# Loads behind the offset conv, the norm's mean and root one product later, and other orders in the first and last slots of a deformable bottleneck

## The chip, the cores and the metric

The kernel runs on one core of a Trainium2 chip. The metric is the device time in microseconds (us) of one execution. TensorE is called PE here, VectorE DVE, ScalarE ACT, GpSimd POOL and SyncE SP, as in the profile. All data are float32.

## The reference, cut to what matters

Two residual bottlenecks run one after the other on x of shape (64, 1024, 14, 14).

```python
# layer 0: batch norms over the whole batch
out = relu(bn(conv1x1(x, w1) + b1))            # 1024 -> 256
out = relu(bn(conv3x3(out, w2) + b2))          # 256 -> 256
x = relu(x + softplus(scale) * bn(conv1x1(out, w3) + b3))
# layer 1: group norms with 32 groups per image, a deformable 3x3 conv
out = relu(gn(conv1x1(x, w1)))                 # 1024 -> 256
om = conv3x3(out, w_off) + b_off               # 27: offsets x, y and a mask, 9 taps each
sampled = bilinear(out, grid + offsets) * sigmoid(mask)     # 9 taps x 256 channels
out = relu(gn(sum over taps of w2[tap] @ sampled[tap]))
return relu(gn(conv1x1(out, w3)) + x)          # 256 -> 1024
```

## The kernel before, in words

Two images make a pair; there are 32 pairs (NP), and a pair's 392 positions are the columns of a matmul. Layer 0 runs until about 967 us and leaves its third conv's results (h3) in DRAM, because its last batch norm needs all pairs. Layer 1 finishes layer 0's last norm, residual and ReLU pair by pair and then does its own work. The change touches layer 1 alone (`build_second_bottleneck`) and a helper for its weights.

Layer 1 is a pipeline over slots. `fill()` (from about 967 us) brings pairs 0 and 1 in and starts pair 2; then `slot(t)` runs for t = 0 to 31, and `tail()` ends pair 31. In slot t the following work of several pairs is laid side by side:

- the first conv of pair t+1 (`first_conv`, L1092, 16 matmuls) with the norm of pair t-1's second conv (`second_norm`) placed between its products, the store of the second half of pair t-2 (`output(t-2, 1)`, L1752), and `load(t+2)`, which issues four DMAs on SP: x into Y[(t+2) % 4] (L196) and h3 into Z0 (L204);
- the sampling of pair t (`sampling`, L1396 on PE, copied by ACT at L1404 into the sample tiles sm_0 with five taps and sm_1 with four), woven with pair t-1's third conv (`third_conv`, L1640), whose sums V, E and z are made by DVE and POOL (L1647 to L1660) and whose last statistics are taken by DVE at L987;
- the offset conv of pair t+1 (`offset_conv`) and `selection` (L1219 to L1234), which ends with DMAs of offsets, weights and mask (dm, wt, mk) through DRAM and back;
- the second conv of pair t (`second_conv`, L1511). It is a 2x2 block product in seven products instead of eight, in the order 5, 0, 4, 1, 2, 3, 6, with five taps in its first part (pd[0], 35 steps) and four in its second (pd[1], 28 steps). A step is one product of 196 columns. DVE makes the differences of sample halves that it needs (L1467): the first (b12 - b11) comes from `first_sum`, tied to program order; three more are issued at steps of the conv. `finish_second` copies the bank E by ACT (L1535), and DVE adds V (L1539) and the outputs h (L1542, 1543, 1549), of which it takes statistics for gn_2.

Between the steps of pd[0] stand, each before a step's number: the mean of pair t-1's third norm at 4, its root at 10 and its scale at 20; `first_sum(t, 0)` at 4 and `first_sum(t, 1)` at 20; the transposes of pair t+1 at 6, 11, 16 and 21 (L1283); its interpolation weights (`factors`, L1246 to L1266, which ends with DMAs wd) at 12 and 19; and `residual(t+2)` at 21 (eight DVE adds at L216 and eight ReLUs of ACT at L228). A norm (`Norm`) is: `total` (m from the statistics, DVE L1003), `mean` (PE L1012, then gm, q and v on DVE, L1014 to L1026), `root` (PE L1031, DVE L1036, a power on POOL L1037) and `scale` (sc, sh; DVE L1043 to L1053). The third norm is then applied to z by ACT in 16 pieces (L1707). In the profile its tiles have the name gn_0, and the norm of the second conv in the next slot has a name with the pair's number, gn_29 for instance.

Two more parts belong to the change. `spread_rows` and `spread_columns` (L1324, L1359) gather wd from DRAM into tiles S and X, and `corners` (L1376) multiplies them on DVE. The last pair (31) uses `plain_second_conv` (L1431), which has two outputs o with two inputs c each, 392 columns, and one difference of a whole sample tile by DVE (L1428) ahead of output 1. In `fill`, `sums_of_second` makes sums of the second conv's weights on DVE (L911).

What sets the order: PE's instructions in layer 1 run in the order in which the code emits them (`tc.manual_schedule` for PE). Lists of steps are put together by `weave` and by `put(steps, extra, at)`, which emits each extra ahead of the step with its number; extras with the same number keep their order in the list after a stable sort. The other engines' order is set by a scheduler, apart from instructions wrapped in `tc.keep_in_program_order`, which stay in the emitted order among each other. A program that also handles far offsets (FULL) is in the kernel, but its branch isn't taken.

Of the kernel before, what the change touches and what calls it, by code (L numbers as in the profile page):

```python
# [20 lines left out]
CB = 8  # L21
HB = CB // 2
MB = 2
T = 9
# [20 lines left out]
def kernel(  # L45
# [854 lines left out]
    Sc = {n: const.tile([P, T, P], FP, tag=f"Sc{n}", name=f"Sc{n}") for n in (1, 2, 4)}  # L900
    Sc[3] = c21

    def sums_of_second():
        for k in range(0, T, 3):
            for n, a, b, op in (
                (1, c21, c22, ALU.add),
                (2, Sc[1], c11, ALU.subtract),
                (3, c11, c21, ALU.subtract),
                (4, c12, Sc[2], ALU.subtract),
            ):  # L910
                nc.vector.tensor_tensor(Sc[n][:, ds(k, 3)], a[:, ds(k, 3)], b[:, ds(k, 3)], op)  # L911


    omax = const.tile([32, NP], FP, tag="omax", name="omax")
# [9 lines left out]
    def build_second_bottleneck(l1, path, run, early):  # L924
# [144 lines left out]
        def load(p):  # L1069
            start(p)  # L1070

            load_x(p, tc.keep_in_program_order)
            load_h3(p, Z0, tc.keep_in_program_order)

        def residual(p):

            for b in range(CB):

                tc.keep_in_program_order(end_of_first(p, Z0, b))
                relu_of_first(p, b)  # L1080
# [251 lines left out]
        def spread_columns(p, e):  # L1332

            q = pairs[p]
            k0, k1 = tapsets[e]
            n = wide * KT[e % 2]
            if shared and p == e == 0:


                first, second = (  # L1340
                    two.tile([P, HB, N2], FP, tag="z", name=f"X_{n}").rearrange("p b n -> p (b n)")
                    for n in range(2)
                )

                cut = [piece for _, _, piece in pieces(e)][-1].start
                where = lambda piece: (
                    second[:QR, : piece.stop - cut] if piece.start == cut else first[:QR, piece]
                )
            elif shared:
                t = sample_buffer(e, f"X_{p}_{e}")  # L1350
                where = lambda piece: t[:QR, piece]
                if e == 1:
                    transformed[p + 1] = t[:, n:]
            else:
                t = one.tile([QR, n], FP, tag=f"X{e % 2}", name=f"X_{p}_{e}")
                where = lambda piece: t[:, piece]
            q["X"][e] = where
            for g, r0, piece in pieces(e):
                yield nc.sync.dma_start(  # L1359
                    where(piece),  # L1360
                    q["wd"][g][1, :, k0:k1, :]
                    .rearrange("r k n -> r (k n)")
                    .unsqueeze(0)
                    .to_broadcast([R, W, piece.stop - piece.start]),
                )
# [49 lines left out]
        def plain_second_conv(p, e):  # L1415


            q = pairs[p]
            k0, k1 = tapsets[e]

            def step(k, o, c):
                sm = q["sm"][e]
                if k == o == c == 0:
                    q["pd"] = [
                        ps_d.tile([P, N2], FP, tag=f"pd{n}", name=f"pd_{p}_{n}") for n in range(MB)
                    ]
                if (k, o, c) == (k0, 1, 0):
                    nc.vector.tensor_tensor(  # L1428
                        sm[:, 1, : k1 - k0], sm[:, 1, : k1 - k0], sm[:, 0, : k1 - k0], ALU.subtract
                    )  # L1430
                nc.tensor.matmul(  # L1431
                    q["pd"][o],
                    ((c11, c12), (Sc[1], c22))[o][c][:, k],
                    sm[:, c, k - k0].rearrange("p i q -> p (i q)"),
                    start=(k == 0 and c == 0),
                    stop=(k == T - 1 and c == MB - 1),
                )
                if k == T - 1 and c == MB - 1:
                    if o == 0:
                        outputs_of_second(p)  # L1440
                    nc.scalar.copy(q["h2"][:, o, :], q["pd"][o])
                    second_stats(p, o)

            return [
                lambda a=(k, o, c): step(*a)
                for o in range(MB)
                for k in range(k0, k1)
                for c in range(MB)
            ]

        def outputs_of_second(p):
            q = pairs[p]
# [13 lines left out]
        def subtract(dst, a, b):  # L1466
            return nc.vector.tensor_tensor(dst, a, b, ALU.subtract)  # L1467
# [12 lines left out]
        def second_conv(p, e):  # L1480
# [49 lines left out]
            def finish_second(m):  # L1530
                bank = q["pd"][m // 2]
                if m == 1:
                    outputs_of_second(p)
                    q["E"] = one.tile([P, 2, HW], FP, tag="E", name=f"E2_{p}")
                    nc.scalar.copy(q["E"], bank)  # L1535
                elif m == 3:
                    V = q["V"] = one.tile([P, 2, HW], FP, tag="V", name=f"V2_{p}")
                    E, h2 = q["E"], q["h2"]
                    nc.vector.tensor_tensor(V, bank, E, ALU.add)  # L1539
                    nc.gpsimd.tensor_tensor(E[:, 1], V[:, 0], E[:, 1], ALU.add)  # L1540
                    nc.gpsimd.tensor_tensor(h2[:, 1, HW:], V[:, 0], V[:, 1], ALU.add)
                    nc.vector.tensor_tensor(h2[:, 1, :HW], bank[:, 1], V[:, 0], ALU.add)  # L1542
                    nc.vector.tensor_tensor(
                        h2[:, 0].rearrange("p (i n) -> p i n", i=2), q["pd"][2], E, ALU.add
                    )
                    second_stats(p, 0)
                elif m == 6:
                    h2 = q["h2"]
                    nc.vector.tensor_tensor(h2[:, 1, :HW], bank[:, 0], h2[:, 1, :HW], ALU.add)
                    second_stats(p, 1)  # L1550
# [232 lines left out]
        def slot(t):  # L1783
# [5 lines left out]
            def part(yes, stage, *args):  # L1789
                return stage(*args) if yes else []  # L1790
# [15 lines left out]
            weights = [lambda e=e: corners(t, e) for e in range(2)] if this else []  # L1806

            late = [lambda: output(t - 2, 1)] if t >= 2 else []
            if t + 2 < NP and not (early and t < 1):
                late.append(lambda: load(t + 2))  # L1810
            if this and not d1 and not early:
                weights[0]()
            if t == NP - 1:
                ends2 = second_norm(t)
            om = part(front, offset_conv, t + 1) + part(front, selection, t + 1)
            half = len(d3) // 2
            if d1:
                extra = list(zip((5, 8, 12, 12, 13, 13, 14), norm2)) + [(10, w) for w in weights[:1]]
# [12 lines left out]
            more = t + 2 < NP and not (early and t < 1)  # L1831

            scale = lambda k: k * len(pd[0]) // 35
            extra = [(4, s) for s in norm3[:1]] + ([(4, lambda: first_sum(t, 0))] if this else [])
            extra += list(zip((6, 11, 16, 21), part(ahead, transposes, t + 1)))
            extra += list(zip((12, 19), part(ahead, factors, t + 1)))
            extra += list(zip((10, 20), norm3[1:]))
            extra += [(20, lambda: first_sum(t, 1))] if this and E == 2 else []
            extra += [(21, lambda: residual(t + 2))] if more else []
            extra = [(scale(k), s) for k, s in extra]  # L1840
# [11 lines left out]
            extra = []  # L1852
            if early and t == 0:

                extra += list(zip((5, 8), first_norm(2)))
            if early and t + 1 in (1, NP - 1):
                extra.append((12, lambda: corners(t + 1, 0)))
            if back:
                extra.append((n * 18 // 28, lambda: output(t - 1, 0)))
            if t == NP - 1:  # L1860

                extra += list(zip([n // 2 + k for k in (3, 5, 6, 6)], ends2))
            extra.sort(key=lambda v: v[0])
            todo += put(pd[E - 1], [s for _, s in extra], [k for k, _ in extra])
            if ahead:
                todo.append(lambda: list(spread_columns(t + 1, 1)))
            if back and t == NP - 1:
                todo.append(lambda: output(t - 1, 1))
            for step in todo:
                step()  # L1870

# [56 lines left out]
        def fill():  # L1928

            for p in range(3):  # L1930
                start(p)
            load_h3(2, Z0)
            steps = first_conv(0, by_inputs=True) + [offset_weights]
            steps += put(
                first_conv(1),
                first_norm(0)
                + offset_conv(0)
                + selection(0)
                + [lambda: pairs[1]["gn1"].total(), lambda: residual(2)]
                + factors(0),  # L1940
                (3, 6, 7, 7, 7, 7) + (12,) * (MB * 3) + (12, 16, 16, 16, 16),
            )
            steps += transposes(0) + [lambda: lend(0)]

            steps += [lambda e=e: list(zip(spread_rows(0, e), spread_columns(0, e))) for e in range(2)]
            steps += put(
                first_conv(2),
                first_norm(1) + [sums_of_second, lambda: corners(0, 0)] + offset_conv(1) + selection(1),
                (1, 4, 7, 7, 8, 8, 11, 11) + (12,) * (MB * 3) + (14,),
            )  # L1950
            for step in steps:
                step()
# [94 lines left out]
```

## Time and profile before

| | us |
|---|---|
| median of 3 runs | 2930.93 (2928.26 to 2932.24) |
| the profiled execution's own time | 2930.46 |
| its span in the profile | 2928.7 |
| PE busy | 2824.3 (96%) |
| DVE busy | 2330.2 (80%) |
| ACT busy | 1336.8 (46%) |
| POOL busy | 988.9 (34%) |

The span is the stretch from the first to the last instruction that the profiler recorded; the execution's own time is 1.8 us longer. A line of the groups, waits and rows below has the engine, the line of the code, the operation, and the tile that it writes and those that it reads. In square brackets stands how long the engine was idle just before, and which engine's instruction ended that. PE's matmuls are pipelined; a float32 product of 196 columns is two records 0.166 us apart, one of 392 columns two records 0.33 apart. The mean granted clock of PE was 0.991 of full speed.

### The profile page before, as it was taken

To read this page: it belongs to the slowest core of one execution; us is meant where nothing else is said; L and a number is where in the kernel's file an instruction comes from. 1 tells how busy PE (TensorE), PEld (TensorE's weight loads), DVE (VectorE), ACT (ScalarE), POOL (GpSimd) and SP (SyncE) were. 2 spreads that over 40 slices of the span, in tenths; PEclk is the share of its full clock that TensorE was granted. 3 is DMA by queue.
4 is the path that set the end of the run, shared out by engine and by line. 5 is a ranking of instruction groups with operands and counts; after the bars stand their busy time and mean duration, and the time that the engine had idled before them with its cause. 6 is when DMAs were issued, how large, how long until landed. Compare 5 with 4: busy or idle time off the path is not lost.

```text
span 2928.7 us, 40983 instructions
## 1 busy us (share of the span) xinstructions
PE 2824.3 (96%) x13327; PEld 2053.4 (70%) x13327; DVE 2330.2 (80%) x5573; ACT 1336.8 (46%) x2723; POOL 988.9 (34%) x1065
## 2 busy tenths in 40 slices
PE   9999899999999889999999999999999999999986
PEld 5555555555555468878887888778877887788773
DVE  7877899997888758778877887787878787877764
ACT  0000222114555435555555556555655565556553
POOL 4621466654666112222222222222222222222221
PEclk9999999999999999999999999999999999999998
DMA  7665000005555444564456545554555455544521
GB/s 229 192 176 154 15 1 1 1 2 213 218 195 203 133 130 138 176 187 160 141 173 184 162 143 168 188 164 144 164 187 169 142 164 185 172 142 159 183 93 46
DMA packets 350436, 424.42 MB, mean 145 GB/s; under 512 B 27876, under 2 KB 292612, under 8 KB 349956
## 3 DMA queue, kind: packets, MB, share of 16 engines
q1 hardware_dynamic: 350212, 421.71, 44.7%
q8 instruction: 107, 1.75, 0.3%
q14 instruction: 117, 0.96, 0.1%
HBM read 296.63 MB, written 116.76 MB: 141 GB/s over the span
## 4 chain that ended last, share of the span: by engine, by line
PE 63%; DVE 19%; DMA 8%; ACT 3%; POOL 3%; issue 2%; SPq 1%; DVEq 0%; ACTq 0%; POOLq 0%
PE pd L1511 18%; PE c L389 10%; PE c L770 9%; PE sp L1396 6%; PE d L1092 6%; PE c L534 5%; DMA out_dram<-z 5%; PE d L1640 4%; DVE v L520 3%; DVE gn_0st L987 2%; DVE S L1376 2%; DMA X<-wd 1%; DVE V L1647 1%; DVE off L1207 1%; DVE X L1156 1%
## 5 line engine op out<-in xcount | busy, mean ns | idle before, releaser
L1396 PE MATMUL sp<-S,aT 126*128 126x420 f32 (+3 forms) x1536 | 494.7, 419 | 22.6 <-ACT sm L1404 13.0
L1511 PE MATMUL pd<-sm,w2b_sb 128*128 128x196 f32 x2232 | 408.6, 331 | 3.8 <-DVE sm L1467 3.8
L1404 ACT COPY sm<-sp 128x336 f32<-128x336 f32 (+3 forms) x640 | 285.6, 451 | 254.5 <-PE sp L1396 239.9
L1511 PEld LDWEIGHTS pd<-sm,w2b_sb 128*128 128x128 f32 x2232 | 370.6, 190 | 4.1 <-DVE sm L1467 4.1
L1092 PE MATMUL d<-h,w1b_sb 128*128 128x392 f32 x1024 | 358.0, 498 | 2.8 <-ACT h L228 2.8
L534 PE MATMUL c<-v,u_sb 128*128 128x392 f32 x1024 | 342.9, 497 | 10.4 <-DVE bn1sh L167 8.2
L1511 PE MATMUL pd<-sm,Sc 128*128 128x196 f32 x1674 | 315.5, 331 | 0.0
L534 PEld LDWEIGHTS c<-v,u_sb 128*128 128x128 f32 x1024 | 194.4, 191 | 158.9 <-DVE v L520 11.7
L1396 PEld LDWEIGHTS sp<-S,aT 126*128 126x128 f32 x1536 | 256.7, 191 | 47.0 <-ACT sm L1404 32.4
L1467 DVE TENSOR_TENSOR sm<-sm 128x980 f32<-128x980 f32 (+1 forms) x248 | 263.4, 1072 | 20.7 <-PE pd L1511 14.6
L1511 PEld LDWEIGHTS pd<-sm,Sc 128*128 128x128 f32 x1674 | 277.9, 190 | 0.2
L1092 PEld LDWEIGHTS d<-h,w1b_sb 128*128 128x128 f32 x1024 | 188.6, 190 | 121.0 <-ACT h L228 5.2
L1707 ACT ACTIVATE z<-z,gn_0sh,gn_0sc 128x196 f32<-128x196 f32 x496 | 222.5, 537 | 36.6 <-DVE gn_0sh L1053 36.6
L1037 POOL TENSOR_TENSOR gn_0sc<-gn_0sc,mhalf 128x16 f32<-128x16 f32 (+3 forms) x35 | 122.1, 3488 | 251.6 <-DVE gn_0sc L1036 242.3
L520 DVE TENSOR_TENSOR v<-t 128x392 f32<-128x392 f32 x256 | 193.1, 812 | 0.0
L1640 PE MATMUL d<-h,w3b_sb 128*128 128x196 f32 x744 | 180.4, 333 | 0.0
L1726 ACT ACTIVATE z<-z 128x784 f32<-128x784 f32 x124 | 103.1, 855 | 145.4 <-DVE z L1724 145.2
L1652 POOL TENSOR_TENSOR E<-V,E 128x196 f32<-128x196 f32 x124 | 74.4, 600 | 281.3 <-DVE V L1647 281.3
L1640 PEld LDWEIGHTS d<-h,w3b_sb 128*128 128x128 f32 x744 | 132.9, 189 | 50.4 <-issue 19.7
L1376 DVE TENSOR_TENSOR S<-S,X 126x840 f32<-126x840 f32 (+1 forms) x192 | 148.3, 822 | 24.1 <-DMA X<-wd 18.7
L1540 POOL TENSOR_TENSOR E<-V,E 128x196 f32<-128x196 f32 x31 | 18.8, 605 | 412.7 <-DVE V L1539 392.7
L987 DVE BATCH_NORM_STATS2 gn_0st<-z 128x6 f32<-128x196 f32 x504 | 153.2, 348 | 4.2 <-ACT z L1691 0.9
(842 smaller groups left out, 5147.3 us busy)
## 6 DMA issues: line engine op xcount, KB each, us to landing
xc<-in_x_dram SPq DMA_DIRECT2D x128, 392.0 KB
h<-o SPq DMA_DIRECT2D x64, 784.0 KB
h<-in_x_dram SPq DMA_DIRECT2D x64, 784.0 KB
h<-h SPq DMA_DIRECT2D x64, 784.0 KB
out_dram<-z SPq DMA_DIRECT2D x126, 392.0 KB
S<-wd SPq DMA_DIRECT2D x64, 413.4 KB
X<-wd SPq DMA_DIRECT2D x64, 413.4 KB
S<-wd SPq DMA_DIRECT2D x64, 330.8 KB
```

The source lines that it names most:

```text
L389: nc.tensor.matmul(acc[m], a, b, start=(j == 0), stop=(j == HB - 1))
L520: nc.vector.tensor_tensor(v[:, u].rearrange("p (i y x) -> p i y x", y=7, x=7), cols[c][:, :, i : i + 13 : 2, :], cols[c][:, :, j : j + 13 ...
L534: nc.tensor.matmul(m[u], u_sb[:, c, u, k % 4, ts(o, P)], vts[k][c][:, u], start=(c == 0), stop=(c == MB - 1),)
L770: nc.tensor.matmul(planes(acc[m]), a, b, start=start, stop=True, skip_group_check=True)
L987: last = nc.vector.bn_stats(self.st[:, b, i, :], src[:, ts(i, HW)])
L1092: nc.tensor.matmul(q["pt"][o], w1b_sb[:, c, ts(o, P)], q["y"][:, c, :], start=(c == 0), stop=(c == CB - 1),)
L1396: nc.tensor.matmul(pt[:, i], q["aT"][:, i0 + i, c, starts.index(r0), :], q["S"][e][g, r0][:, :, i0 + i, :], start=(j == 0), stop=(j == len ...
L1404: nc.scalar.copy(dst, pt.rearrange("p i k n -> p k i n"))
L1467: return nc.vector.tensor_tensor(dst, a, b, ALU.subtract)
L1511: nc.tensor.matmul(bank[:, m % 2], a[:, k], b[:, k - k0],  start=(k == 0 and m in (5, 0, 2, 6)), stop=(k == T - 1), skip_group_check=True,)
L1640: nc.tensor.matmul(bank[:, m % 2 if m < 6 else 1], a, b, start=(m < 6), stop=True, skip_group_check=True)
L1707: nc.scalar.activation(z[:, ts(i, HW)], z[:, ts(i, HW)], AF.Identity, bias=n.sh[:, b, i : i + 1], scale=n.sc[:, b, i : i + 1],)
```

## The change

1. `load(t+2)` moves from the extras of the first conv to the end of the list of the offset conv and the selection, so that its four DMAs stand on SP behind those of dm, wt and mk.
2. In pd[0] the third norm's mean moves from step 4 to step 5 where the slot has a first conv (t = 2 to 30) and to 8 where not; the root stands five steps after it.
3. In slots 0 and 30 (`bare`) the factors go from steps 12 and 19 to 4 and 10, `corners(t+1, 0)` in pd[1] from 12 to six before the end, and in slot 0 a root of `first_norm(2)` from 8 to 11. V's add on DVE is tied to program order for pairs 0 and 30.
4. In `fill`, the weight sums are made in two parts, each tied to program order; the offset conv's weights, the norm of pair 1 and the residual of pair 2 (in three pieces) are emitted at other places; and the last gathered piece of pair 0's second tap set goes into an unused part of another buffer.
5. The last pair's whole-tile difference becomes one difference for each tap, issued when output 0's product of that tap has been issued; output 1 takes the taps of input 0 first and then those of input 1. Pair 30's two stores go to other steps.

```diff
-    def sums_of_second():
-        for k in range(0, T, 3):
+    def sums_of_second(*ks):
+        for k in ks:
...
-                nc.vector.tensor_tensor(Sc[n][:, ds(k, 3)], a[:, ds(k, 3)], b[:, ds(k, 3)], op)
+                tc.keep_in_program_order(
+                    nc.vector.tensor_tensor(Sc[n][:, ds(k, 3)], a[:, ds(k, 3)], b[:, ds(k, 3)], op)
+                )
...
-        def residual(p):
-            for b in range(CB):
+        def residual(p, b0=0, b1=CB):
+            for b in range(b0, b1):
...
+                q["spare"] = second[:QR, wide * KT[0] - cut :]
             elif shared:
...
+                spare = q.get("spare") if e == 1 else None
+                where = lambda piece: (
+                    spare[:, : piece.stop - piece.start]
+                    if spare is not None and piece == last
+                    else t[:QR, piece]
+                )
...
-                if (k, o, c) == (k0, 1, 0):
-                    nc.vector.tensor_tensor(
-                        sm[:, 1, : k1 - k0], sm[:, 1, : k1 - k0], sm[:, 0, : k1 - k0], ALU.subtract
-                    )
...
+                if (o, c) == (0, 1):
+                    subtract(sm[:, 1, k - k0], sm[:, 1, k - k0], sm[:, 0, k - k0])
...
+            order = [(k, 0, c) for k in range(k0, k1) for c in range(MB)]
+            order += [(k, 1, c) for c in range(MB) for k in range(k0, k1)]
+            return [lambda a=a: step(*a) for a in order]
...
-                    nc.vector.tensor_tensor(V, bank, E, ALU.add)
+                    tie = tc.keep_in_program_order if p in (0, NP - 2) else lambda v: v
+                    tie(nc.vector.tensor_tensor(V, bank, E, ALU.add))
...
-            if t + 2 < NP and not (early and t < 1):
-                late.append(lambda: load(t + 2))
+            loads = [lambda: load(t + 2)] if t + 2 < NP and not (early and t < 1) else []
...
-            om = part(front, offset_conv, t + 1) + part(front, selection, t + 1)
+            om = part(front, offset_conv, t + 1) + part(front, selection, t + 1) + loads
...
-            extra = [(4, s) for s in norm3[:1]] + ([(4, lambda: first_sum(t, 0))] if this else [])
+            bare = early and t + 1 in (1, NP - 1)
+            m = 5 if d1 else 8
+            extra = [(m, s) for s in norm3[:1]] + ([(4, lambda: first_sum(t, 0))] if this else [])
             extra += list(zip((6, 11, 16, 21), part(ahead, transposes, t + 1)))
-            extra += list(zip((12, 19), part(ahead, factors, t + 1)))
-            extra += list(zip((10, 20), norm3[1:]))
+            extra += list(zip((4, 10) if bare else (12, 19), part(ahead, factors, t + 1)))
+            extra += list(zip((m + 5, 20), norm3[1:]))
+            if back and t == NP - 1:
+                extra.append((32, lambda: output(t - 1, 0)))
...
-                extra += list(zip((5, 8), first_norm(2)))
-            if early and t + 1 in (1, NP - 1):
-                extra.append((12, lambda: corners(t + 1, 0)))
-            if back:
+                extra += list(zip((5, 11), first_norm(2)))
+            if bare:
+                extra.append((n - 6, lambda: corners(t + 1, 0)))
+            if back and t < NP - 1:
                 extra.append((n * 18 // 28, lambda: output(t - 1, 0)))
+            elif back:
+                extra.append((3, lambda: output(t - 1, 1)))
...
-            steps = first_conv(0, by_inputs=True) + [offset_weights]
+            steps = first_conv(0, by_inputs=True)
+            norm = first_norm(0)
             steps += put(
                 first_conv(1),
-                first_norm(0)
-                + offset_conv(0)
-                + selection(0)
-                + [lambda: pairs[1]["gn1"].total(), lambda: residual(2)]
-                + factors(0),
-                (3, 6, 7, 7, 7, 7) + (12,) * (MB * 3) + (12, 16, 16, 16, 16),
+                norm[:2] + [offset_weights] + norm[2:] + offset_conv(0) + selection(0),
+                (3, 5, 5, 6, 6, 6, 6) + (12,) * (MB * 3) + (12,),
             )
-            steps += transposes(0) + [lambda: lend(0)]
+            norm, (distances, end) = first_norm(1), factors(0)
+            steps += [lambda: pairs[1]["gn1"].total(), lambda: residual(2, 0, 3)] + transposes(0)
+            steps += norm[:1] + [lambda: residual(2, 3, 7), distances, lambda: residual(2, 7), end]
+            steps += [lambda: lend(0)]
...
-                first_norm(1) + [sums_of_second, lambda: corners(0, 0)] + offset_conv(1) + selection(1),
-                (1, 4, 7, 7, 8, 8, 11, 11) + (12,) * (MB * 3) + (14,),
+                norm[1:]
+                + [lambda: sums_of_second(0, 3), lambda: corners(0, 0)]
+                + offset_conv(1)
+                + selection(1)
+                + [lambda: sums_of_second(6)],
+                (3, 7, 7, 8, 8, 11, 11) + (12,) * (MB * 3) + (14, 16),
```

## The prediction

> **What bounds the kernel now.** I read the page's busy shares first, then TensorE's waits in the steady slots (1130 to 2700 us), then one slot instruction by instruction, then the waits outside the steady slots. Busy shares:
>
> ```profile
> PE 2824.3 (96%) x13327; PEld 2053.4 (70%) x13327; DVE 2330.2 (80%) x5573; ACT 1336.8 (46%) x2723; POOL 988.9 (34%) x1065
> ```
>
> TensorE (PE) works 96% of 2928.7 us, so only what makes PE wait, or slows its clock, can move the time. The waits of the steady slots (total, times, longest), first PE's, then the largest one of VectorE (DVE):
>
> ```profile
> PE gn_0p L1012 <- DVE gn_0m L1003: 8.3, 27, 0.3
> PE sp L1396 <- ACT sm L1404: 7.1, 27, 0.3
> PE d L1640 <- DVE z L1656: 6.5, 10, 1.2
> ```
>
> ```profile
> DVE V L1539 <- ACT E L1535: 43.4, 26, 1.7
> ```
>
> A slot takes 58.8 us (gn_0m at 1157.2 and 26 slots on at 2687.1). PE loses about 22 us in 27 slots, little each time, and always to something DVE or ScalarE (ACT) delivers just in time. DVE itself stands still 1.67 us in each slot until ACT has copied E. Here is the slot that ends at 2767 us; start, length, engine, instruction, idle before. DVE:
>
> ```profile
> 2745.18 0.63 DVE L987 BATCH_NORM_STATS2 gn_0st<-z 128x6 f32<-128x196 f32 x2
> 2745.84 0.19 DVE L1003 TENSOR_TENSOR gn_0m<-gn_0st 128x16 f32<-128x16 f32 x1
> 2746.51 0.17 DVE L1014 COPY gn_0gm<-gn_0p 128x16 f32<-128x16 f32 x1 [0.49 <-PE gn_0p L1012]
> ...
> 2747.56 0.18 DVE L1026 TENSOR_TENSOR gn_0v<-gn_0q 128x16 f32<-128x16 f32 x1
> 2747.65 2.46 DVE L1467 TENSOR_TENSOR sm<-sm 128x980 f32<-128x980 f32 x2
> 2750.02 0.17 DVE L1036 TENSOR_SCALAR gn_0sc<-gn_0p 128x16 f32<-128x16 f32 x1
> 2750.14 1.18 DVE L1467 TENSOR_TENSOR sm<-sm 128x980 f32<-128x980 f32 x1
> 2751.24 0.99 DVE L1246 TENSOR_TENSOR wt<-wt,base_sb 126x784 f32<-126x784 f32 x1
> 2752.15 1.17 DVE L1467 TENSOR_TENSOR sm<-sm 128x980 f32<-128x980 f32 x1
> 2754.12 0.25 DVE L1043 TENSOR_TENSOR gn_0sc<-gn_0sc,vec 128x8 f32<-128x8 f32 x2 [0.81 <-POOL gn_0sc L1037]
> ```
>
> ACT, and PE at the two means:
>
> ```profile
> 2754.87 7.18 ACT L1707 ACTIVATE z<-z,gn_0sh,gn_0sc 128x196 f32<-128x196 f32 x16 [0.87 <-DVE gn_0sh L1053]
> ...
> 2762.21 4.21 ACT L228 ACTIVATE h<-h,bn3sh 128x392 f32<-128x392 f32 x8
> 2766.32 0.47 ACT L1535 COPY E<-pd 128x392 f32<-128x392 f32 x1
> ```
>
> ```profile
> 2746.08 0.40 PE L1012 MATMUL gn_0p<-gn_0m,grp_sb 128*128 128x16 f32 x2 [0.31 <-DVE gn_0m L1003]
> ```
>
> ```profile
> 2770.38 0.33 PE L1012 MATMUL gn_29p<-gn_29m,grp_sb 128*128 128x4 f32 x2
> ```
>
> The reader is to see one chain: last statistics of z, m, PE's mean, v, PE's root, GpSimd's power (3.82 us), scale and shift, ACT's 16 normalisations, its 8 ReLUs, its copy of E, then DVE's V and the statistics of the second conv, and PE's mean of those (gn_29p). From 2754.87 to 2766.79 ACT has no gap. m of gn_29 is at 2770.10 and PE's mean starts 0.28 later, just as its previous matmul leaves (2768.07 plus seven at 0.33 is 2770.39). The same distance of 0.3 to 0.4 us stands between that m and that matmul for pairs 5 to 21. So the chain has no slack: what delays z's shift delays PE in the next slot.
>
> Outside the steady slots three PE waits stand out:
>
> ```profile
> 1064.51 2.12 PE L1511 MATMUL pd<-sm,w2b_sb 128*128 128x196 f32 x8 [3.80 <-DVE sm L1467]
> ```
>
> ```profile
> 2832.91 4.36 PE L1396 MATMUL sp<-S,aT 126*128 126x420 f32 x6 [7.18 <-DVE h L1542]
> ...
> 2870.59 1.23 PE L1431 MATMUL pd<-sm,w2b_sb 128*128 128x392 f32 x2 [2.09 <-DVE sm L1428]
> ```
>
> **What the Trainium skill says.** "PSUM — Partial Sum Buffer", section "Engine vs sequencer instructions": VectorE's and ScalarE's queues are strictly first in, first out, and matmuls start in program order. The trace agrees: DVE idles 0.81 us at L1043 with differences queued behind it. So an instruction put ahead of m delays m by its whole length. "DMA: Bandwidth & Descriptors", section "Issuing engines are not separate DMA queues": all transfers share 16 engines and interleave. The trace agrees: z's adds wait 11.9 us in 18 slots for out_dram stores, which run beside the loads. "TensorE: Matmul & The Clock Gate", section "What's actually happening": the clock halves after an idle window of about 3.4 us. Here idle of 2.09 us is followed by matmul steps of 1.0 to 1.3 us where 0.66 is usual; after idle of 1.41 us or less I find no slow ones.
>
> **The change, part by part.** The sum starts from the profiled run's 2930.46 us (span 2928.7 and 1.8 around it); the median of the three runs is 0.5 above.
>
> *Steady slots (t = 2 to 29, 28 slots).* Nominally the norm's mean moves one product later (4 to 5), one matmul step of 0.33 us (two records 0.166 apart), which would more than cover the 0.31 us stall. But the first difference of the sampled halves keeps its place at 4 and is tied to program order. It is thus now issued ahead of m, and the order of DVE's instructions in the built program shows it: BATCH_NORM_STATS, difference, m, difference, gm, ..., v, difference, sc, wt, half of the scale, difference, other half, shift. Before, m followed the statistics directly and no difference stood between the halves. With a spacing of 1.10 us for a difference (2750.14 to 2751.24):
> - m: 2745.84 + 1.10 = 2746.94. PE's mean 0.24 later, 2747.18. PE comes there at 2745.77 + 0.33 = 2746.10: a stall of 1.08 instead of 0.31. PE alone: 0.77 later.
> - gm: PE's result would be there at 2747.6, but the second difference runs until 2748.2; v 1.05 later (as before), 2749.25.
> - PE's root: PE comes at 2748.62 + 0.77 = 2749.39, v is done at 2749.43: about even.
> - Third difference 2749.5 to 2750.6 (it needs the product that PE finishes at about 2749.5); sc at 2750.6 (before 2750.02), so the power ends 0.58 later and the first half of the scale is 0.58 later.
> - Fourth difference between the halves: 1.10 more. z's shift, and ACT's start, come 0.58 + 1.10 = 1.68 us later.
> - ACT is without gap, so E, V, gn_2's m and PE's mean are 1.68 later; PE had lost 0.77, and waits the other 0.9 there. DVE's tail has cover: it idled 1.67 before V, and E moves by as much as the work does. The second half's differences (2760.45) stay about 0.5 us ahead of their products.
> Per slot +1.68; 28 slots: **+47.0 us**. Bounds: +0.77 (only PE's own loss; 21.6) to +1.9 (PE restarts a little slowly; 53).
>
> *Loads moved behind the offset conv's transfers.* dm, wt and mk go first, so they lose nothing; the loads start at about 2743 instead of 2718.6 and last 5.59 + 2.89 = 8.5 us, so they land at about 2751.5 to 2754.5. What is queued behind them on SyncE is wd, at 2754.03 (later in the new order). DMA is idle from 2744 to 2754. Their readers, the ReLU input adds, begin at 2756.14 + 1.68. Cover 3 to 6 us; without it each us of lateness is one for DVE. The stores at the slot's start now run alone: the z adds' wait goes, and with it PE's 6.5 us at L1640. Value −6.5, bounds 0 and −8.
>
> *Slot 1.* Mean at 8, root at 13; three differences of 1.10 stand ahead of the shift: **+3.3** (0 to +4).
>
> *Fill and slot 0.* Statistics of pair 1 earlier, weight sums split and tied, residual in pieces, a separate place for the last gathered piece, V tied ahead. PE waits 2.73 (gn_1v at 1005.04), 2.08 (S at 1017.74), 2.75 (sm at 1031.59), 3.80 and 1.41 us here. I take the second conv of slot 0 to begin 5 us earlier, and 3.80 plus 1.41 to go; a little new waiting on gn_1 is inside my range. **About −11** (−6 to −13).
>
> *Slot 30.* The factors and gather weights come earlier (4, 10), so S doesn't wait 5.06 us for its gather ahead of V; V is tied ahead of S. The 7.18 us stall largely goes; but m is behind two differences and the weights, about 3.1 us late, of which PE loses 2.6. **−4.5** (0 to −6).
>
> *Last pair.* Two whole differences (128x1960 and 128x1568) become nine of 128x392 in step with the first output's taps; DVE's elements are the same. The 2.09 and 1.23 us stalls go, with some 1.8 us of slow matmuls; the stores of pair 30 leave earlier. **−5.5** (−2 to −9).
>
> Sum: 47.0 − 6.5 + 3.3 − 11 − 4.5 − 5.5 = +22.8; 2930.46 + 22.8 = 2953.3, and 2953.7 from the median; I say **2953.5**.
>
> **The rivals.**
> B, the other side: ACT's chain has slack that one slot's rows hide, and only PE's own stall counts. Then 28 x 0.77 = 21.6, slot 1 +1.5, the rest −27.5: −4.4, 2926. The deciding point is whether V's m comes later than PE at the gn_2 mean; if its slack were over 0.9 us, this case holds. For it: no wait there is listed for PE. Against: the 0.3 us from m to matmul in slot after slot.
> C: the move does what its index says; DVE finds a gap for the first difference (as at the 0.49 us idle ahead of gm), m isn't later, and the 0.31 us stalls vanish: 28 x −0.31 − 27.5 = −36, 2894. Against: the queue's order.
> D: the loads come late as well, since wd and the gather share their transfers; the ReLU adds hold DVE for 1 us in each slot: 2953.5 + 28 = 2981. Against: the DMA gap of 10 us.
>
> **How the numbers follow.** Mine 0.72, B 0.15, C 0.05, D 0.08. Mine with its bounds runs from 2935 to 2968 (28 slots at 1.2 to 1.9, ends −20 to −31). The range leaves out C, about half of B and two thirds of D: 2925 to 2974. About 0.2%, 5.9 us, is what a measurement of this kernel can tell from no change. Slower by more: nearly all of mine and D, 0.75; within: the low edge of mine and half of B, 0.11; faster: C, the other half of B, 0.14.
>
> **What would show it.** Right: PE waits of about 1.1 us for gn_0m in 28 slots, and of about 0.9 at gn_2's mean; ACT's normalisation 1.7 us later against the second conv's start; slots of 60.5 us instead of 58.8; no z wait on out_dram; no 7.18 and 3.80 us waits. Wrong: gn_2's mean without a wait, or slots of 58.8 or less; or adds L216 that wait for the loads.

## The result, and the profile after

The changed kernel takes 2945.89 us (median of 5 runs, 2941.81 to 2947.81), the kernel before 2928.26 us (median of 5 runs, 2927.09 to 2932.24). The ratio is 1.0054, with a 95% interval from 1.0039 to 1.0069: 17.6 us slower, where 2953.5 and 22.8 us slower were forecast. The profiled execution of the changed kernel took 2947.35 us, with a span of 2945.5.

The waits of TensorE in the steady slots of the changed kernel (total, times, longest):

```profile
PE gn_0p L1015 <- DVE gn_0m L1006: 25.1, 27, 0.9
PE sp L1407 <- ACT sm L1415: 6.6, 27, 0.3
PE d L1649 <- DVE z L1665: 4.7, 7, 1.1
PE gn_2p L1015 <- DVE gn_2m L1006: 0.3, 1, 0.3
```

and the largest wait of VectorE there:

```profile
DVE gn_0sc L1046 <- POOL gn_0sc L1040: 72.9, 26, 2.8
```

The wait for the third norm's m has gone from 0.31 to 0.93 us in every slot, and at the second norm's mean (gn_2p here, and likewise for the other pairs) a new one of 0.3 us has come. VectorE now stands still for 2.8 us in a slot ahead of the scale. One slot, VectorE's rows:

```profile
2771.99 0.63 DVE L990 BATCH_NORM_STATS2 gn_0st<-z 128x6 f32<-128x196 f32 x2
2772.53 1.16 DVE L1474 TENSOR_TENSOR sm<-sm 128x980 f32<-128x980 f32 x1
2773.61 0.18 DVE L1006 TENSOR_TENSOR gn_0m<-gn_0st 128x16 f32<-128x16 f32 x1
2773.80 1.18 DVE L1474 TENSOR_TENSOR sm<-sm 128x980 f32<-128x980 f32 x1
2774.89 0.17 DVE L1017 COPY gn_0gm<-gn_0p 128x16 f32<-128x16 f32 x1
...
2776.25 1.18 DVE L1474 TENSOR_TENSOR sm<-sm 128x980 f32<-128x980 f32 x1
2777.35 0.17 DVE L1039 TENSOR_SCALAR gn_0sc<-gn_0p 128x16 f32<-128x16 f32 x1
2777.43 0.96 DVE L1249 TENSOR_TENSOR wt<-wt,base_sb 126x784 f32<-126x784 f32 x1
2781.20 0.17 DVE L1046 TENSOR_TENSOR gn_0sc<-gn_0sc,vec 128x8 f32<-128x8 f32 x1 [2.80 <-POOL gn_0sc L1040]
2781.28 1.17 DVE L1474 TENSOR_TENSOR sm<-sm 128x980 f32<-128x980 f32 x1
2782.37 0.16 DVE L1046 TENSOR_TENSOR gn_0sc<-gn_0sc,vec 128x8 f32<-128x8 f32 x1
```

The first difference stands ahead of m, and the fourth stands at 2781.28 between the two halves of the scale, where VectorE had just been idle for 2.8 us: it could have run in that gap, but its place in the queue is behind the first half. The chain of waits of the changed kernel, over one slot, followed back from the end; start, length, what:

```profile
2712.28 0.63 DVE gn_0st L990 x2
2712.90 1.08 DVE sm L1474
2714.13 0.40 PE gn_0p L1015 x2
...
2717.88 3.58 POOL gn_0sc L1040
...
2725.98 4.51 ACT z L1716 x10
2730.49 0.26 ACT aT L1289
2730.75 4.11 ACT h L228 x8
2734.86 0.38 ACT E L1542
2735.27 0.58 DVE V L1548
...
2738.77 0.39 PE gn_28p L1015 x2
```

This is the chain that the prediction named, now on the path that set the end: before, that path went through TensorE's products in this stretch:

```profile
2753.32 13.93 PE pd L1511 x84
2767.25 3.29 PE d L1092 x10
2770.54 0.17 PE gn_29p L1012 x2
```

From the chain I take the landmarks of a slot, as means over slots 4 to 27, in us from the second conv's first product; the last column is the time from slot to slot.

| kernel | last statistics | m | PE's mean | PE's root | sc | ACT's z | PE's gn_2 mean | slot |
|---|---|---|---|---|---|---|---|---|
| before | 0.90 | 1.56 | 1.80 | 4.34 | 5.74 | 10.59 | 26.09 | 58.81 |
| changed | 0.89 | 2.52 | 2.75 | 5.08 | 6.26 | 11.94 | 27.38 | 60.02 |

m is 0.96 later, sc 0.52, ACT's normalisation 1.35, PE's next mean 1.29, and a slot 1.21 us longer.

### The profile page after: what moved, and what is told of

Read it like the earlier page. It is cut to its first block, busy times and chain, and to the rows that moved or that the text cites. A ratio compares the mean times of both kernels' runs of the same rounds, so it can differ in the third digit from the quotient of the medians.

```text
span 2945.5 us, 40897 instructions
## 1 busy us (share of the span) xinstructions
PE 2831.3 (96%) x13327; PEld 2053.2 (70%) x13327; DVE 2325.2 (79%) x5580; ACT 1329.5 (45%) x2723; POOL 978.7 (33%) x1065
## 4 chain that ended last, share of the span: by engine, by line
PE 49%; DVE 20%; ACT 14%; POOL 6%; issue 6%; DMA 4%; SPq 0%; DVEq 0%; POOLq 0%; ACTq 0%
PE c L389 10%; PE c L770 9%; PE sp L1407 7%; ACT z L1716 7%; PE c L534 6%; PE d L1649 5%; PE d L1095 5%; ACT h L228 4%; POOL gn_0sc L1040 4%; DVE v L520 3%; DMA out_dram<-z 2%; DVE gn_0st L990 2%; PE pd L1518 2%; DVE sm L1474 2%; DVE V L1656 1%
## 5 line engine op out<-in xcount | busy, mean ns | idle before, releaser
L1518 PE MATMUL pd<-sm,Sc 128*128 128x196 f32 x1674 | 308.1, 329 | 0.0
L1474 DVE TENSOR_TENSOR sm<-sm 128x980 f32<-128x980 f32 (+2 forms) x257 | 268.1, 1053 | 22.9 <-PE pd L1518 13.9
L1040 POOL TENSOR_TENSOR gn_0sc<-gn_0sc,mhalf 128x16 f32<-128x16 f32 (+3 forms) x35 | 113.1, 3233 | 263.4 <-DVE gn_0sc L1039 254.1
L1387 DVE TENSOR_TENSOR S<-S,X 126x840 f32<-126x840 f32 (+1 forms) x192 | 147.7, 819 | 12.0 <-DMA X<-wd 11.9
```

The lines of the kernel that those rows point to most:

```text
L1040: nc.gpsimd.tensor_tensor(scf, scf, mhalf[:, :U], ALU.pow)
L1518: nc.tensor.matmul(bank[:, m % 2], a[:, k], b[:, k - k0],  start=(k == 0 and m in (5, 0, 2, 6)), stop=(k == T - 1), skip_group_check=True,)
```

## The experiments

All ran against the kernel before; ratios are to that, with 95% intervals. The kernel before had medians of 2933 to 2936 us then, so I compare ratios, and inside a slot the landmarks.

**The mean back at 4.**

```diff
-            m = 5 if d1 else 8
+            m = 4 if d1 else 8
-            extra += list(zip((m + 5, 20), norm3[1:]))
+            extra += list(zip((10 if d1 else m + 5, 20), norm3[1:]))
```

> The changed kernel with the third norm's mean back at step 4 and its root at 10 in the slots that have a first conv (t = 2 to 30); everything else as changed. In the built program m stands directly behind the last statistics again, and the first difference after v. Theory (the difference ahead of m, and the one between the scale's halves, cost 1.16 us in each of 27 slots): 2945.9 - 27 x 1.16 - about 1 in slot 30 = 2913, range 2909 to 2918; no gn_0m wait over 0.4 us in the steady slots; slots of 58.8 us. Rival (the loads behind the offset conv, or something else of the change, makes the slots longer): slots stay near 60.0 us and the time over 2938.

Measured: 2906.89 us, ratio 0.9903 (0.9885 to 0.9921). Waits of TensorE in the steady slots of this kernel:

```profile
PE gn_0p L1015 <- DVE gn_0m L1006: 8.3, 27, 0.3
PE sp L1407 <- ACT sm L1415: 6.2, 27, 0.3
PE d L1649 <- DVE z L1665: 2.8, 4, 1.8
```

The wait for m is as in the kernel before, and the landmarks too. One number in the list of steps turns a loss of 0.54% into a gain of 0.97%. A slot takes 58.52 us, so the late mean costs 60.02 - 58.52 = 1.50 us, not the 1.21 by which slots differ from before; the other changes give 0.29 back, all of it after gn_2's mean, and the run with the moved loads alone below shows that they do it. Of the 1.50 us, 1.29 are there at gn_2's mean. That is why the time fell below the expected 2909 to 2918: I had taken the net as the cost.

**The mean at 5 alone, in the kernel before.**

```diff
-            extra = [(4, s) for s in norm3[:1]] + ([(4, lambda: first_sum(t, 0))] if this else [])
+            m = 5 if d1 else 4
+            extra = [(m, s) for s in norm3[:1]] + ([(4, lambda: first_sum(t, 0))] if this else [])
```

> The kernel before, with nothing but the third norm's mean moved from step 4 to 5 in the slots with a first conv. Theory: the whole loss of the steady slots without the gains of the other parts: 2928.3 + 27 x 1.16 + 1 to 3 in slot 30 = 2961, range 2956 to 2966. Rival (the loss comes from the mean together with the moved loads): under 2945.

Measured: 2973.41 us, ratio 1.0132 (1.0112 to 1.0152), some 39 us; a slot of 60.35, 1.54 more than before. The 39 us are just over the 28 to 38 by which the expected range lay above the kernel before, for the same reason. 27 slots of 1.50 are 40.5 us.

**The first difference behind the mean.**

```diff
-            ... [(4, lambda: first_sum(t, 0))] if this else [])
+            ... [(m, lambda: first_sum(t, 0))] if this else [])
```

> The changed kernel with the mean at step 5 as changed, and the first difference emitted behind it at the same step (in slot 1 and 31 at the mean's step too). In the built program the order is statistics, m, difference, gm. Theory (order on VectorE decides, not the step on TensorE): as with the mean at 4, and TensorE's stall of 0.31 us is covered by the step moved ahead: 2913 - 27 x 0.31 = 2905, range 2901 to 2914; gm about 0.6 us later against the start of the second conv, but sc earlier since only one difference stands ahead of it. Rival (a later mean is what costs): near 2946.

This kernel changes part of the computation: b22's difference is formed from b12 before the first difference has been taken from it, so that products of the second conv have other values. The instructions and their sizes are the same. Measured: 2900.91 us, ratio 0.9883 (0.9866 to 0.9900), slots of 58.51: a mean at step 5 costs nothing once m isn't queued behind a difference. It also gains nothing in a slot, which isn't as expected: the stall of 0.31 us ahead of the mean is gone, but TensorE then waits for v. It starts the root at 4.22 us, where it does at 4.01 in the run below with VectorE's order tied, and the products behind the root stand where they stood with the mean at 4.

**The scale's halves together.**

```diff
+                    tie = tc.keep_in_program_order if nb == CB else lambda v: v
-                    nc.vector.tensor_tensor(
+                    tie(nc.vector.tensor_tensor(
                         sc[:, :, i], sc[:, :, i], vec[:, self.scol : self.scol + nb], ALU.mult
-                    )
+                    ))
...
-                    subtract(b21, b21, b22)
+                    tc.keep_in_program_order(subtract(b21, b21, b22))
```

> The changed kernel with the fourth difference (b21) and the scale's two halves of the third norm tied to program order, so that no difference stands between the halves; m stays behind the first difference. Theory (chain to z's shift decides beyond TensorE's own loss): ScalarE's normalisation starts about 0.8 us earlier against the second conv's start, and what remains is TensorE's own loss of 0.7 us in each slot: 2945.9 - 27 x 0.45 = 2934, range 2928 to 2939. Rival (only m's delay and TensorE's stall cost, the chain over ScalarE has slack): within 2 us of 2946. Second rival (only the halves cost): 2915.

Measured: 2922.15 us, ratio 0.9956 (0.9941 to 0.9971), slots of 59.21. VectorE's rows:

```profile
2753.04 0.96 DVE L1250 TENSOR_TENSOR wt<-wt,base_sb 126x784 f32<-126x784 f32 x1
2754.17 1.18 DVE L1475 TENSOR_TENSOR sm<-sm 128x980 f32<-128x980 f32 x1 [0.16 <-PE pd L1519]
2755.95 0.57 DVE L1257 TENSOR_TENSOR wt<-wt,mk 126x392 f32<-126x392 f32 x1 [0.60 <-ACT wt L1252]
2756.81 0.24 DVE L1047 TENSOR_TENSOR gn_0sc<-gn_0sc,vec 128x8 f32<-128x8 f32 x2 [0.29 <-POOL gn_0sc L1040]
```

The fourth difference now runs while GpSimd makes the power, and the halves follow each other. So the loss has two parts: 0.81 us of the 1.50 come from the difference between the halves, and 0.69 are left, with m as late as in the changed kernel. Of the 0.81, 0.44 are there at gn_2's mean (26.94 instead of 27.38); the rest comes later in the slot, some 0.1 of it where TensorE waits for z, and no run takes it apart. Neither rival alone holds. The time is lower than expected since the whole was 1.50.

**Two differences ahead of m.**

```diff
+                tie = tc.keep_in_program_order if self.nb == CB else lambda v: v
-                nc.vector.tensor_tensor(self.m, st[:, :, 1], st[:, :, 4], ALU.add)
+                tie(nc.vector.tensor_tensor(self.m, st[:, :, 1], st[:, :, 4], ALU.add))
...
-                    subtract(b22, b22, b12)
+                    tc.keep_in_program_order(subtract(b22, b22, b12))
```

> The changed kernel with m tied behind two differences instead of one; in the built program none stands between the scale's halves now. m comes 1.08 us later still (3.6 us after the second conv's start), the scale's end and ScalarE's normalisation 0.4 to 0.8 us earlier than in the changed kernel. Theory (a slot loses the larger of two delays: TensorE's own, from m, and the chain's over ScalarE): TensorE's own is 0.7 + 1.1 = 1.8 us and decides, so a slot of 60.3 us and about 8 us more than the changed kernel: 25 us over the kernel before, range 15 to 32. Rival (only the chain to z's shift counts): 10 to 20 us less than the changed kernel, 0 to 8 over the kernel before. Second rival (the delays add): 27 x 1.1 = 30 us more than the changed kernel, 47 over the kernel before.

Measured: 2986.51 us, ratio 1.0187 (1.0173 to 1.0201), slots of 61.44: 55 us over the kernel before, near the second rival and far from my own number. TensorE's rows of one slot:

```profile
2806.39 1.82 PE L1519 MATMUL pd<-sm,Sc 128*128 128x196 f32 x10
2810.43 0.40 PE L1016 MATMUL gn_0p<-gn_0m,grp_sb 128*128 128x16 f32 x2 [2.21 <-DVE gn_0m L1007]
2810.67 0.58 PE L1519 MATMUL pd<-sm,w2b_sb 128*128 128x196 f32 x2
2811.08 0.58 PE L1287 MATMUL tr<-ident,a 128*126 128x128 f32 x2
2811.46 2.82 PE L1519 MATMUL pd<-sm,w2b_sb 128*128 128x196 f32 x8
2814.08 0.44 PE L1035 MATMUL gn_0p<-gn_0v,grp_sb 128*128 128x16 f32 x2
2814.36 0.66 PE L1519 MATMUL pd<-sm,w2b_sb 128*128 128x196 f32 x2
2814.86 0.38 PE L1287 MATMUL tr<-ident,a 128*126 128x128 f32 x2
2815.08 1.49 PE L1519 MATMUL pd<-sm,w2b_sb 128*128 128x196 f32 x8
```

After 2.21 us without work, eight records (four products) take 2.82 us where 1.49 is usual (last line): the matmuls run at half their rate for about 3 us, and the granted clock that the trace records is 0.5 there. This isn't so in each slot. Of slots 4 to 28, 17 have such a stretch; the other eight have the same idle of 2.21 us and keep their clock:

| slots | TensorE's root | ACT's z | gn_2's mean | slot |
|---|---|---|---|---|
| kernel before | 4.34 | 10.59 | 26.09 | 58.81 |
| two ahead, full clock (8) | 6.24 | 12.13 | 28.00 | 60.26 |
| two ahead, half clock (17) | 7.79 | 13.69 | 29.65 | 61.93 |

With the full clock my number held: TensorE's delay at the root is 1.90 us where I had 1.8, and a slot takes 60.26 us where I had 60.3. What I had left out is the clock, which adds 1.67 us in two slots of three: the third difference waits for the slow products (2.24 us in the slot shown), which makes sc and z late too. So the nearness to the second rival, that delays add, is chance. The larger of two delays fits all four cases to about 0.1 us: TensorE's root and ACT's z are 0.74 and 1.35 later than before in the changed kernel (gn_2's mean 1.29 later), 0.74 and 0.26 with the halves together (0.85), 1.90 and 1.54 here with the full clock (1.91), 3.45 and 3.10 with half of it (3.56). I formed that rule before this run, but its numbers are read off afterwards, and z comes later here than the 11.94 us of the changed kernel, where I had expected it earlier.

**The other parts alone.** Each is the kernel before with the lines of the diff for this part only: the loads (part 1), the fill with slot 0 (part 4 and slot 0's share of 3), and slots 30, 31 and the tail (part 5 and slot 30's share of 3).

> The kernel before with nothing but the loads moved behind the transfers of dm, wt and mk. Theory: between the changed kernel with its mean at 4 and the kernel before, a steady slot differs by 0.29 us (58.52 and 58.81), all of it between the second conv's norm and the next second conv; 27 slots: 7.8 us less than before, range 3 to 11; the z adds' waits for stores go from 18 to under 10. Rival (the loads cost time, and the other parts hide it): 0 or slower.

Measured: 2918.96 us, ratio 0.9947 (0.9934 to 0.9960), 15.5 us less: twice what was expected. Slots take 58.47 us. VectorE's wait for the stores in the kernel before, and then with the loads moved:

```profile
DVE z L1656 <- DMA out_dram<-z: 11.9, 18, 1.6
```

```profile
DVE z L1656 <- DMA out_dram<-z: 5.7, 10, 1.8
```

In the two kernels below, which have the loads at their old place, that wait was 21.4 and 18.0 us, and TensorE's at L1653 and L1638 behind it 13.9 and 12.5 us instead of the 6.5 of the kernel before. So the gain of a slot is 0.34 us against the profile before (58.81 - 58.47) and 0.57 against the kernel with the last slots' changes alone (59.04 - 58.47). I take the difference to lie in how loads and stores meet from run to run; the kernel before was not profiled again, so that isn't shown.

> The kernel before with nothing but the changes to the fill and to slot 0 (weight sums in parts, order of the norm and the residual, the spare place, the factors of slot 0 at 4 and 10, corners late, V of pair 0 tied). Theory: the means of slots 0 and 1 came 5.4 to 6.9 us earlier in the kernels with all parts, so 6 us less than before, range 3 to 9; a wait of about 5 us for S at the first sampling stays. Rival (11 us, as the prediction had it).

Measured: 2930.01 us, ratio 0.9981 (0.9974 to 0.9988), 5.6 us less, as expected.

> The kernel before with nothing but the changes to slots 30, 31 and the tail (last pair's differences tap by tap, factors of slot 30 at 4 and 10, corners late, V of pair 30 tied, stores of pair 30 earlier). Theory: from slot 29 to the end the changed kernel gains 11.0 us on the kernel before and the one with the mean at 4 gains 11.5; so 11 us less, range 8 to 14. Rival (the prediction's 10 us was 4.5 plus 5.5 and slot 30's late mean took some): here, with the mean at 4, up to 14.

Measured: 2924.30 us, ratio 0.9966 (0.9953 to 0.9979), 10 us less, as expected.

**VectorE's order tied.** The sum at the mean's step is issued between m and gm, and b22's difference behind v; the norm's instructions and the differences are tied in the order in which they are emitted.

```diff
-            extra = [(m, s) for s in norm3[:1]] + ([(4, lambda: first_sum(t, 0))] if this else [])
+            extra = [(m, lambda: pairs[t - 1]["gn3"][0].total())] if norm3 else []
+            extra += [(m, lambda: first_sum(t, 0))] if this else []
+            extra += [(m, s) for s in norm3[:1]] + ([(m, lambda: second_sum(t))] if this else [])
...
+        def second_sum(p):
+            if sevenfold(p):
+                b12, b22 = (pairs[p]["sm"][0][:, c, :, 1] for c in range(2))
+                tc.keep_in_program_order(subtract(b22, b22, b12))
```

> The changed kernel with mean at 5 and root at 10, but VectorE's order around it tied: m, first difference, gm, q, v, second difference, sc, third difference, fourth, both halves of the scale, shift; the first two differences at the mean's step in slot 1 too. Same work and same result as the changed kernel. Theory (order on VectorE decides, and a steady slot can't be shorter than about 58.5 us since the kernels with m at its old place agree there, though z's shift is 0.6 us earlier in one of them): a steady slot of 58.5 us as with the mean at 4, and 2 to 5 us less than that in all because of slot 1: 28 to 34 us under the kernel before. Rival (TensorE's mean at step 5 costs in itself): 10 us or more above the kernel with the mean at 4.

Measured: 2893.86 us, ratio 0.9856 (0.9842 to 0.9871), better than expected. Slots take 58.23 us, 0.29 less than with the mean at 4, and no wait for m is left in the steady slots: the first difference runs while TensorE makes the mean, and the extra step covers the stall of 0.31. The root follows at 4.01 us, where it had to wait for v until 4.22 with the first difference merely behind the mean; the gain is kept here.

**Corners behind V.** In that kernel, corners of slots 0 and 30 go from n - 6 to n - 4.

> The kernel with VectorE's order tied around a mean at step 5 (the fastest so far), with corners of the next pair in slots 0 and 30 two steps later (four before the end of the second conv's second part), so that V and the outputs stand ahead of the corner products on VectorE, and these wait for their gather behind V. Theory (in slot 0 and 30 of the changed kernel V was queued behind corner products that waited 3.4 + 1.3 us for the gather, but the gather itself lands so late that the next sampling, which reads the products, can't begin much earlier): the waits for h of 3.5 and 4.2 us become waits for S, and the time falls by 0 to 3 us. Rival (V's place is what costs): 6 to 8 us less.

Measured: 2890.47 us, ratio 0.9853 (0.9840 to 0.9866), the same as the version it starts from within the intervals: the median is 3.4 us lower, but so was that of the kernel before, by 2.6. TensorE in slot 1's sampling waits 2.51 us for S where it had waited 3.53 for h. The gather's landing decides there, as expected; whether anything of the whole time was gained is open. These two are the fastest versions, 1.5% under the kernel before.

## Why the prediction was right

The direction, the place and the chain were right, and each link shows in the trace. Point by point:

- *m behind the first difference*: forecast 1.10 us later, measured 0.96; TensorE's stall 1.08, measured 0.93. Right.
- *sc*: forecast 0.58 later, measured 0.52. Right.
- *The difference between the halves*: forecast 1.10 on top, measured 0.83. VectorE's spacing is as forecast (2781.28 to 2782.37 is 1.09), but GpSimd's power became shorter, 3.57 instead of 3.82 us. So z's shift is 1.35 late, not 1.68.
- *No slack over ACT*: right. E follows ACT's start by 11.45 us and V follows E by 0.50 in both kernels, and gn_2's mean is 1.29 late. TensorE was to be 0.9 us later there than by its own loss; it is 0.44 later than with the halves together, where nothing waits, and 0.28 of that is listed as a wait. z's delay was smaller than forecast, and TensorE's own loss up to there larger, 0.85 instead of 0.77.
- *The sum*: the mean's move cost 1.50 us per slot against 1.68, 40 us against 47. Rival B falls with the halves kept together, which shorten a slot by 0.81 us though m is as late, and rival C with the statistics' row followed by the difference. D falls too: the loads made slots shorter.
- *Loads*: forecast -6.5 with a lower bound of -8. Against the kernel before in its own profile the slots gain 27 x 0.29 = 7.8, but the part alone gained 15.5. The bound was mis-sized: it came from the waits in a single profile, and in the two other kernels with the loads at their old place what TensorE loses by them is twice as long. The waits were also forecast to go, and they only became less: z's adds wait 6.8 us in 9 slots for the stores instead of 11.9 in 18, and TensorE's wait for z fell from 6.5 to 4.7 us.
- *Fill*: forecast -11, measured -5.6. The first half held: the second conv's w2b products begin at 1033.7 instead of 1039.6. What failed is the other half, that the 3.80 and 1.41 us "go". They did, but a wait in their place came:

```profile
1055.21 1.03 DVE L1387 TENSOR_TENSOR S<-S,X 126x840 f32<-126x840 f32 x1 [3.35 <-DMA X<-wd]
...
1058.02 1.03 DVE L1387 TENSOR_TENSOR S<-S,X 126x840 f32<-126x840 f32 x1 [1.27 <-DMA X<-wd]
1058.97 0.56 DVE L1548 TENSOR_TENSOR V<-pd,E 128x392 f32<-128x392 f32 x1
```

```profile
1060.07 4.37 PE L1407 MATMUL sp<-S,aT 126*128 126x420 f32 x6 [4.98 <-DVE h L1551]
```

  VectorE's rows and TensorE's next row in slot 0: V is *behind* the corner products. I had written "V tied ahead"; a tie keeps the emitted order, and corners at six before the end are emitted ahead of step 22 of the 28, V with step 23.
- *Slots 30, 31*: forecast -4.5 and -5.5. The changed kernel gains 11.0 from slot 29's mean (27.8 us late) to the end of its span (16.8 late), so the sum held, but 0.6 of it falls between the means of slots 29 and 31 and 10.4 after. The 7.18 us stall fell to 0.74, as forecast; but m is late in slot 30, and its stall of 2.90 us is followed by 6.8 us at half the clock. What the last pair gains is more than I took.
- *Slot 1*: forecast +3.3; from slot 1's mean to slot 2's it is 61.53 against 59.44 us, +2.1.

In the profiles of the two kernels the stretches add up: -5.6 us to slot 1's mean, +2.1 in slot 1, +31.3 in the 27 slots from slot 2's mean to slot 29's, -11.0 from there on, together +16.8. Forecast were -11, +3.3, +40.5 (47.0 - 6.5) and -10. So the steady slots were taken 9 us too dear and the fill 5 us too good, and that these errors cancel in part, so that 22.8 is as near to 17.6 as it is, is luck.

The parts alone add up to -31 us and the late mean to +39, so +8, where +17.6 was measured. Most of the gap is in what they are compared with: the median of the kernel before was 2928.3 us beside the changed kernel and 5 to 8 us higher beside the parts. Why it was higher isn't shown; slots of 59.02 and 59.04 us in the two kernels with the loads at their old place, against 58.81 in the profile before, point to the waits for the stores. The mean's cost is thus known to some 5 us: 38.7 alone in the kernel before, 39.0 between the medians of the changed kernel and the one with the mean at 4, 44 between their ratios, 40.5 by slots.

## What to carry to other kernels

When two steps are emitted at neighbouring places, moving one past the other changes the queue of every engine that both feed, not only of the engine whose step was to be moved. Here a step of 0.33 us on TensorE put a difference of 1.10 us ahead of a sum of 0.19 us that a whole chain waits for. Read the built order of the other queues before you price such a move, and then follow the chain behind it to the first wait that has slack.

## What the runs showed of the hardware

GpSimd's power on 128x16 had three lengths. It took 3.82 us in 30 of 31 slots of the kernel before, where VectorE had just begun a difference (128x980, 1.18 us); 3.57 in 28 of 31 slots of the changed kernel, where it had just begun an addition for the interpolation weights (126x784, 0.96); and 2.91 in the others, where VectorE ran nothing. So it was longer by 0.91 and 0.66 us, where 1.05 and 0.80 us of VectorE's instruction were left to run. The Trainium skill ("SBUF — State Buffer", "Who interferes with whom") says that a VectorE instruction with two SBUF inputs contends with a GpSimd instruction that reads SBUF, which agrees. Only the instruction under way at the start counted in these traces: in the kernel before, two more of VectorE's with two SBUF inputs ran inside the power at their usual length, and in slot 1 of the kernel with the halves together a difference of 1.18 us began 0.5 us into a power that still took 2.91. No run was made to vary this alone.

TensorE's granted clock halved after idle of 2.21 us in most slots with two differences ahead, less than the window of about 3.4 us that the prediction cited, and after 2.90 us in slot 30 of the changed kernel, but not after 0.93. The length of the idle doesn't settle it: with two differences ahead, eight of slots 4 to 28 kept the full clock after 2.21 us, and slot 30 after 2.90. In that trace every half-clock stretch begins on a grid of 3.41 us. I sum up TensorE's idle in each such window from the matmul records, from 1000 us on: after a window at full clock with 2.07 us of idle or more, the next ran at half clock; after one with 2.00 or less it didn't. So an idle that two windows share can pass without harm. The other traces have such a limit too, each at a somewhat different place: in all of them it lies between 1.8 and 2.1 us.
